# Fills between vector passes, and three groups of gathered lists beside the batches instead of two

## The chip, the core and the metric

The kernel runs on one core of a Trainium2 chip. The metric is the time of one execution on the device in microseconds (us), from the first to the last instruction of the core and what little lies around it. Five engines work side by side, each in the fixed order of its own queue, and wait for one another through semaphores: TensorE (PE, with its weight loads as PEld), VectorE (DVE), ScalarE (ACT), GpSimd (POOL) and SyncE (SP). SP issues the plain transfers of this kernel, POOL all indirect ones: a gather or scatter whose rows are named by a list of indices.

## What is computed

There are 16 graphs with 1024 nodes and 64 channels. `adj` is a dense weighted adjacency in which about 1 in 256 entries is not zero, far more in the first rows than in the last.

```python
# layer 0
h = relu(layernorm(x))
x = x + (adj / max(rowsum(adj), 1)) @ h
# layer 1
h = relu(layernorm(x))
nb = (adj > 0) without the diagonal;  m = nb.sum(-1)
# a node with more than 10 neighbours drops those whose rank is a multiple of ceil(m/2), in both directions
valid = nodes that are left, the node itself among them
agg[c] = 0.25*quantile(h[valid, c], .25) + 0.5*quantile(.., .5) + 0.25*quantile(.., .75)
out = x + (relu((h + agg) @ W1 + b1) @ W2 + b2) * mask
```

The quantiles need each node's neighbours in sorted order, channel by channel.

## The kernel before

**Layer 0, the batches.** For each graph (`front`, then `back`) SP loads eight blocks of 128 rows of `adj`, DVE turns each block into the numbers of its nonzero columns (`max` over four segments, L336), PE transposes it (L341) and multiplies it with `h` (L358). `back` writes the layer's result to two tables in DRAM (`tab` and `own`), and ranks the nodes of the graph by list length with a one-hot permutation (L438, L444), so that lists of like length lie together. The result of four graphs is one record, `rec_g`.

**Layer 1, the groups.** Four graphs make a group, and there are four groups. A group's 4096 nodes lie in 32 tiles of 128 lists. `group` first prepares: it transposes the records, finds keys and indices of every list, gathers one row of `adj` for tile 0 (`gat_rows`), and writes which neighbours the longest lists drop into the table (`tab`, L757). It then makes one job for each class of list length (`CAPS`): ten jobs of 1 to 6 tiles, with 15, 10, 8, 7, 6, 5, 4, 3, 2 and 1 neighbours. A job goes through four steps. `fetch` gathers its rows on POOL, one indirect transfer for each neighbour of each tile (`places`, L481) and one for the node itself (`S`, L481). `sort` runs on DVE: a sorting network of elementwise minimum and maximum between places (L531), then a product with the quantile weights (L544). `layers` is the small perceptron on PE and ACT, which ends in the tile `y` (L590, two buffers). `add` adds the residual on DVE (L629), and `store` scatters `y` to the output, again on POOL (L595). In `pipeline` step s fetches job s+2 (`AHEAD`), stores job s-2, runs the perceptron of job s-1 and sorts job s. Over its ten jobs a group issues 124 gathers of neighbours, 31 of own rows and 31 stores.

**The longest lists.** The 32 longest lists of every graph (tile 0 of the groups) go separately, in four jobs over all graphs, with eight lists of each graph in a job: `long_lists` finds up to 88, 31, 24 and 20 neighbours from whole rows of `adj` (`lat`), and their rows come into `lplaces`.

**The order of work.** The program is written as generators. Each `yield` names a cost, and `weave` always advances the stream that has used the smaller part of its budget; `WAIT` says that a stream can't go on yet. Before, a first stage weaves the batches (budget 480) with groups 0 and 1 (budget 270), where a job's costs are DVE's time. A second stage weaves the longest lists (440) with groups 2 and 3 (270); all four `long_lists` are prepared before the first of their jobs is fetched. A group may start when the fronts of its graphs are written. What the generators write out is then arranged by a scheduler, which gives each engine its fixed order: an instruction without a dependency can stand far ahead of where it was written.

The lines that matter in the profile are these: L481 all gathers, L595 the stores, L491 the first instruction of a sort (`rem`), L531 the passes of the network, L544 the products, L590 and L629 the end of a job.

Of the kernel before, what the change touches and what calls it, by code (L numbers as in the profile page):

```python
# [10 lines left out]
I32 = mybir.dt.int32  # L11
# [24 lines left out]
LONG = (88, 31, 24, 20)  # L36
LSUB = 8
WAIT = "wait"
AHEAD = 2


# [110 lines left out]
def list_path(ctx, tc, x, adj, nodemask, w1, b1, w2, b2, out, go):  # L152
# [24 lines left out]
    ps_s = ctx.enter_context(tc.tile_pool(name="ps_s", bufs=3, space=bass.MemoryType.PSUM))  # L177


    diff = consts.tile([P, P], I32, name="diff")  # L180
    nc.gpsimd.iota(diff, pattern=[[1, P]], base=0, channel_multiplier=-1)
    ident = consts.tile([P, P], F32, name="ident")
    nc.vector.tensor_scalar(ident, diff, 0.0, None, op0=OP.is_equal)
# [17 lines left out]
    nc.vector.tensor_scalar(rev, col, -1.0, float(N), op0=OP.mult, op1=OP.add)  # L201
    zeros = consts.tile([P, N], BF, name="zeros")
    nc.vector.memset(zeros, 0.0)
    place1 = consts.tile([P, P], F32, name="place1")
    nc.vector.tensor_scalar(place1, col[:, :P], 1.0, None, op0=OP.add)
    cls_i = consts.tile([P, CLS, NT], I32, name="cls_i")
    nc.gpsimd.iota(cls_i, pattern=[[-1, CLS], [0, NT]], base=CLS - 1, channel_multiplier=0)
    cls = consts.tile([P, CLS, NT], F32, name="cls")
    nc.vector.tensor_copy(cls, cls_i)
# [41 lines left out]
    adj_rows = adj.rearrange("b i j -> (b i) j")  # L251
    out_rows = out.rearrange("b n c -> (b n) c")

    first = keep.tile([REC, len(LONG), B, LSUB], HF, name="first")
    scatters = []

# [229 lines left out]
    def aggregate(pool, n, T, A, S, keys, node):  # L486

        rem = pool.tile([P, n - 1, T, 2], F32, name="rem2")  # L490
        nc.vector.tensor_tensor(  # L491
            rem, A[:, 1:, :, C:],
            node.unsqueeze(1).unsqueeze(3).to_broadcast([P, n - 1, T, 2]), OP.is_equal,
        )
        gone = pool.tile([P, n - 1, T], F32, name="gone")
        nc.vector.tensor_tensor(gone, rem[:, :, :, 0], rem[:, :, :, 1], OP.max)
        ok = pool.tile([P, n - 1, T], F32, name="ok")
        nc.vector.scalar_tensor_tensor(
            ok, keys.rearrange("p t k -> p k t"), 0.0, gone, op0=OP.is_gt, op1=OP.subtract
        )  # L500
        valid = pool.tile([P, T], F32, name="valid")
        nc.vector.tensor_reduce(valid, ok.rearrange("p k t -> p t k"), AX.X, OP.add)
        ops, count, at = network(n)
        w = weights(pool, count, T, valid)
        vals = A[:, 1:, :, :].rearrange("p k t w -> p (k t) w")[:, :, :C]
        nc.vector.scalar_tensor_tensor(
            vals, gone.rearrange("p k t -> p (k t)").unsqueeze(2).to_broadcast([P, (n - 1) * T, C]),
            HUGE, vals, op0=OP.mult, op1=OP.add,
        )
        Bt = pool.tile([P, n, T, C], F32, name="other", bufs=1)  # L510

        def places(copy, start, step, number):
            if copy == 2:
                return S[:, :, :C].unsqueeze(1)
            src = A if copy == 0 else Bt
            return src[:, start:start + step * (number - 1) + 1:step, :, :C]

        cost = 2.0 + (n - 1) * T * C * 1.05e-3
        for op, ai, aj, dist, run in ops:
            if cost > 8.0:  # L520
                yield cost
                cost = 0.0
            cost += 0.15 + len(run) * T * C * 1.05e-3
            step = run[1] - run[0] if len(run) > 1 else 1
            a = places(ai, run[0], step, len(run))
            c = places(aj, run[0] + dist, step, len(run))
            if op == OP.min:
                dst = places(0 if ai == 1 else 1, run[0], step, len(run))
            else:
                dst = places(0 if aj == 1 else 1, run[0] + dist, step, len(run))  # L530
            nc.vector.tensor_tensor(dst, a, c, op)  # L531

        short = pool is gat
        total = max(count + 1, 4)
        if short:
            prod = pool.tile([P, T, total, C], F32, name="prod", bufs=2)
            if count + 1 < total:
                nc.vector.memset(prod[:, :, count + 1:, :], 0.0)
        for copy in range(2):
            for run in runs_of([k for k in range(count) if at[k] == copy]):  # L540
                step = run[1] - run[0] if len(run) > 1 else 1
                sl = slice(run[0], run[-1] + 1, step)
                src = places(copy, run[0], step, len(run))
                nc.vector.tensor_tensor(  # L544
                    prod[:, :, sl, :].rearrange("p t k c -> p k t c") if short else src, src,
                    w[:, sl, :].unsqueeze(3).to_broadcast([P, len(run), T, C]), OP.mult,
                )
        yield cost + 0.4 + count * T * C * 1.05e-3
        if not short:
            return [  # L550
                [places(at[k], k, 1, 1)[:, 0, t, :] for k in range(count)] + [S[:, t, :C]]
                for t in range(T)
            ]
        nc.scalar.copy(prod[:, :, count, :], S[:, :, :C])

        return [
            [prod[:, t, k:min(k + 2, total), :].rearrange("p k c -> p (k c)")
             for k in (0, *range(4, total, 2), 2)]
            for t in range(T)
        ]  # L560

    def perceptron(terms, mask, T):

        R = terms[0][0].shape[1]
        y = mlp.tile([P, T, CO], F32, name="y", bufs=2)
        for t0 in range(0, T, 4):
            ts = range(t0, min(t0 + 4, T))
            M = len(ts) * P
# [62 lines left out]
        def store(self):  # L631
            store(self.y, self.T, self.nodes_i)

    def pipeline(jobs, ahead):

        J = len(jobs)
        for j in range(min(ahead, J)):
            jobs[j].fetch()
        for s in range(J + 2):
            if s + ahead < J:  # L640
                jobs[s + ahead].fetch()
            if s >= 2:
                jobs[s - 2].store()
            if 1 <= s <= J:
                jobs[s - 1].layers()
            if s < J:
                yield from jobs[s].sort()
            if 1 <= s <= J:
                jobs[s - 1].add()
            yield 0.2  # L650

    def group(g, rec_g):

# [227 lines left out]
    def groups(records, gs):  # L881
        for g in gs:
            while progress["batches"] < (g + 1) * GB:
                yield WAIT
            yield from group(g, records[g])
            yield from pipeline(todo[g], AHEAD)

    def longs(pool):
        for l in range(len(LONG)):
            yield from long_lists(pool, l)  # L890
        while not progress["dropped"]:
            yield WAIT
        yield from pipeline(todo[NG], 2)

    records = []
    with tc.tile_pool(name="lay0", bufs=2) as pool:
        lay0 = batches(pool, records)
        while progress["batches"] < GB - 1:
            next(lay0)
        weave((lay0, 480.0), (groups(records, (0, 1)), 270.0))  # L900
    with tc.tile_pool(name="long", bufs=1) as pool:
        def rest():
            yield from group(2, records[2])
            yield from group(3, records[3])
            progress["dropped"] = True
            yield from pipeline(todo[2] + todo[3], AHEAD)
        weave((longs(pool), 440.0), (rest(), 270.0))


    bad = tiny.tile([P, 1], F32, name="bad")  # L910
# [288 lines left out]
```

## Time and profile before

| | us |
|---|---|
| median of 3 runs (2073.25 to 2082.36) | 2081.86 |
| the profiled execution's own time | 1907.73 |
| its span | 1905.9 |
| DVE busy / POOL busy | 1277.7 / 1183.2 |
| PE busy / PEld busy / ACT busy | 852.7 / 520.7 / 434.3 |
| indirect transfers on POOL: `places`, `lplaces`, `S` of groups, stores of groups | 496, 163, 124, 124 |
| preparation of groups 0, 1, 2 and 3 begins on DVE | 176, 514, 878, 911 |
| first sort of the 88-neighbour lists begins | 1126 |

A group of the profile lists its busy time, its mean duration in ns, and the idle time of the engine ahead of it with what ended that wait. A row of the stage table shows the busy time of each engine in a stretch of the span, with the number of instructions in brackets. A timeline line has its start, its duration, the engine, the source line and, in square brackets, the idle time before it. The busy time of a POOL transfer is its issue on the engine, not the flight of the data.

### The profile page before, as it was taken

To read this page: it belongs to the slowest core of one execution; us is meant where nothing else is said; L and a number is where in the kernel's file an instruction comes from. 1 tells how busy PE (TensorE), PEld (TensorE's weight loads), DVE (VectorE), ACT (ScalarE), POOL (GpSimd) and SP (SyncE) were. 2 spreads that over 40 slices of the span, in tenths; PEclk is the share of its full clock that TensorE was granted. 3 is DMA by queue.
4 is the path that set the end of the run, shared out by engine and by line. 5 is a ranking of instruction groups with operands and counts; after the bars stand their busy time and mean duration, and the time that the engine had idled before them with its cause. 6 is when DMAs were issued, how large, how long until landed. Compare 5 with 4: busy or idle time off the path is not lost.

```text
span 1905.9 us, 15523 instructions
## 1 busy us (share of the span) xinstructions
PE 852.7 (45%) x3724; PEld 520.7 (27%) x3724; DVE 1277.7 (67%) x4747; ACT 434.3 (23%) x1010; POOL 1183.2 (62%) x940
## 2 busy tenths in 40 slices
PE   6898177578973756794002000011163123311275
PEld 4433043245531433452002000011033123301244
DVE  8989799777878998786975036066564776624362
ACT  6654243344441543332000000000001000000021
POOL 0001665775428277744157787788888888878753
PEclk9989587878886787796555555555555556655556
DMA  5645343354342544311111101111111000010100
GB/s 177 184 133 129 96 117 110 94 140 109 96 124 62 144 124 122 84 41 50 37 28 26 27 21 24 27 23 21 21 25 21 14 13 20 14 28 16 27 24 15
DMA packets 116516, 124.32 MB, mean 65 GB/s; under 512 B 84242, under 2 KB 84370, under 8 KB 116418
## 3 DMA queue, kind: packets, MB, share of 16 engines
q1 hardware_dynamic: 85730, 84.15, 15.7%
q0 software_dynamic: 30688, 39.11, 10.0%
q8 instruction: 31, 0.51, 0.1%
q14 instruction: 67, 0.55, 0.1%
HBM read 106.27 MB, written 16.92 MB: 65 GB/s over the span
## 4 chain that ended last, share of the span: by engine, by line
POOL 37%; PE 19%; issue 17%; DVE 15%; DMA 10%; ACT 3%; POOLq 0%; SPq 0%; DVEq 0%; ACTq 0%
POOL places L481 19%; POOL lplaces L481 9%; PE pm L358 6%; POOL S L481 6%; DMA places<-tab,idx 4%; PE pm L444 3%; PE pt L572 3%; POOL out_dram L595 3%; PE pt L341 3%; DMA at<-in_adj_dram 2%; DVE other L531 2%; DVE rec L336 2%; DVE places L531 2%; DMA S<-own,nodes_i 1%; PE ps_small L588 1%
## 5 line engine op out<-in xcount | busy, mean ns | idle before, releaser
L481 POOL DMA_INDIRECT places<-tab,idx x496 | 664.6, 1340 | 214.2 <-issue 140.8
L572 PE MATMUL pt<-ident,prod 128*128 128x128 f32 (+1 forms) x736 | 159.1, 376 | 652.1 <-DVE prod L544 652.1
L572 PEld LDWEIGHTS pt<-ident,prod 128*128 128x128 f32 (+1 forms) x736 | 128.4, 257 | 687.6 <-DVE prod L544 460.6
L358 PE MATMUL pm<-att,h 128*65 128x512 f32 x512 | 244.8, 624 | 6.4 <-ACT att L342 6.4
L595 POOL DMA_INDIRECT out_dram<-y,nodes_i x124 | 131.2, 1058 | 135.2 <-issue 44.6
L481 POOL DMA_INDIRECT S<-own,nodes_i x124 | 189.1, 1525 | 38.4 <-issue 30.2
L481 POOL DMA_INDIRECT lplaces<-tab,lidx x163 | 171.1, 1050 | 49.7 <-issue 49.1
L336 DVE MAX8 rec<-sg 128x8 f16<-128x256 f16 x512 | 188.5, 412 | 1.8 <-issue 1.8
L341 PE MATMUL pt<-ident,at 128*128 128x128 f32 x1024 | 163.0, 306 | 48.3 <-DMA at<-in_adj_dram 30.2
L331 ACT ACTIVATE sg<-at 128x1024 f16<-128x1024 f32 x128 | 135.9, 1061 | 136.7 <-DVE rec L336 124.2
L341 PEld LDWEIGHTS pt<-ident,at 128*128 128x128 f32 x1024 | 132.6, 158 | 85.0 <-issue 41.6
L590 ACT ACTIVATE y<-ps_small,recs 128x64 f32<-128x64 f32 x124 | 30.8, 315 | 535.7 <-DMA out_dram<-y,nodes_i 496.1
L342 ACT COPY att<-pt 128x512 f32<-128x512 f32 x256 | 140.1, 590 | 26.8 <-PE pt L341 25.3
L629 DVE TENSOR_TENSOR y<-y,S 128x64 f32<-128x64 f32 (+4 forms) x44 | 15.0, 343 | 171.3 <-ACT y L590 171.3
L476 DVE TENSOR_TENSOR w<-wu 128x16 f32<-128x16 f32 (+12 forms) x44 | 7.7, 175 | 173.4 <-ACT wu L473 173.4
L481 POOL DMA_INDIRECT gat_rows<-in_adj_dram,nodes_i x4 | 4.4, 1098 | 181.7 <-DVE over L686 176.7
L444 PE MATMUL pm<-perm,rec 128*34 128x512 f16 x256 | 94.2, 482 | 47.7 <-DVE perm L438 46.7
L579 PE MATMUL pm<-ot,w_sb 128*128 128x128 f32 (+3 forms) x112 | 50.5, 551 | 136.0 <-ACT ot L577 136.0
L358 PEld LDWEIGHTS pm<-att,h 128*65 128x65 f32 x512 | 69.8, 144 | 145.1 <-issue 131.4
L531 DVE TENSOR_TENSOR other<-places 128x128 f32<-128x128 f32 (+6 forms) x276 | 91.9, 348 | 0.0
L531 DVE TENSOR_TENSOR other<-lplaces 128x128 f32<-128x128 f32 (+9 forms) x267 | 88.8, 373 | 0.0
L333 DVE TENSOR_TENSOR sg<-sg,rev 128x1024 f16<-128x1024 f16 x128 | 86.9, 681 | 0.0
(194 smaller groups left out, 1671.3 us busy)
## 6 DMA issues: line engine op xcount, KB each, us to landing
at<-in_adj_dram SPq DMA_DIRECT2D x128, 512.0 KB
places<-tab,idx POOLq DMA_INDIRECT x496, 2.5
tab<-h SPq DMA_DIRECT2D x16, 264.0 KB
xt<-in_x_dram SPq DMA_DIRECT2D x16, 256.0 KB
own<-x SPq DMA_DIRECT2D x16, 256.0 KB
own<-h SPq DMA_DIRECT2D x16, 256.0 KB
lplaces<-tab,lidx POOLq DMA_INDIRECT x163, 2.4
S<-own,nodes_i POOLq DMA_INDIRECT x124, 2.6
```

The source lines that it names most:

```text
L331: nc.scalar.activation(sg, at, AF.Sign, accum_out=total[:, t:t + 1])
L333: nc.vector.tensor_tensor(sg, sg, rev, OP.mult)
L336: nc.vector.max(out=rec[:, t, 8 * s:8 * s + 8], in_=segs[:, s, :])
L341: nc.tensor.transpose(pt[:, q * P:(q + 1) * P], at[:, c0:c0 + P], ident)
L342: nc.scalar.copy(att[:, h2 * BPH:(h2 + 1) * BPH, k * P:(k + 1) * P], pt.rearrange("p (q i) -> p q i", i=P),)
L358: nc.tensor.matmul(po[:C + 1, :], st["h0"][:, q, :], st["att"][hf][:, q, :], start=(q == 0), stop=(q == NT - 1),)
L444: nc.tensor.matmul(pr[:REC, :], rec[:, t, :], perm[:, t, :], start=(t == 0), stop=(t == NT - 1))
L481: nc.gpsimd.indirect_dma_start(out=dst, out_offset=None, in_=src, in_offset=bass.IndirectOffsetOnAxis(ap=idx, axis=0),)
L531: nc.vector.tensor_tensor(dst, a, c, op)
L572: nc.tensor.matmul(pt[:term.shape[1], i * P:(i + 1) * P], term, ident, start=(k == 0), stop=(k == len(terms[t]) - 1),)
L579: nc.tensor.matmul(ph[:, :M], w1_sb[:R, :], ot[:R, :M], start=True, stop=True)
L595: ins = nc.gpsimd.indirect_dma_start(out=out_rows, out_offset=bass.IndirectOffsetOnAxis(ap=idx[:, t:t + 1], axis=0), in_=y[:, t, :], in_of ...
```

## The change

Four things are changed.

1. `Breath`: after every 0.8 us of two-operand passes in `aggregate` (L531, L544), as estimated from their sizes, a `memset` of one element in each partition of a tile `idle` of its own is written out on DVE.
2. `pipeline` names other costs: for the groups 1.27 for each indirect transfer that a step issues and nothing for the sort. The long lists keep DVE's costs.
3. The first stage weaves the batches (480) with groups 0, 1 and 2 (730). The second stage has group 3 alone (250) beside the longest lists (440). The 88-neighbour job is fetched as soon as its lists are found and all dropped neighbours are written; the other three `long_lists` are prepared after that.
4. Buffers: `y` has three instead of two. The constants `diff` and `cls_i` share the buffers of `keys` and `idx`, and `place1` becomes a view of `col_f`.

```diff
+BREATH = 0.8
...
-    diff = consts.tile([P, P], I32, name="diff")
+    diff = grp.tile([P, P], I32, name="keys")
...
-    place1 = consts.tile([P, P], F32, name="place1")
-    nc.vector.tensor_scalar(place1, col[:, :P], 1.0, None, op0=OP.add)
-    cls_i = consts.tile([P, CLS, NT], I32, name="cls_i")
+    place1 = col_f[:, 1:]
+    cls_i = grp.tile([P, CLS, NT], I32, name="idx")
...
+    idle = consts.tile([P, 1], F32, name="idle")
+    class Breath:
+        def __init__(self):
+            self.since = 0.0
+        def __call__(self, cost):
+            self.since += cost
+            if self.since > BREATH:
+                nc.vector.memset(idle, 0.0)
+                self.since = 0.0
+    breathe = Breath()
...
             nc.vector.tensor_tensor(dst, a, c, op)
+            breathe(0.07 + len(run) * T * C * 1.05e-3)
...
                     w[:, sl, :].unsqueeze(3).to_broadcast([P, len(run), T, C]), OP.mult,
                 )
+                breathe(0.07 + len(run) * T * C * 1.05e-3)
...
-        y = mlp.tile([P, T, CO], F32, name="y", bufs=2)
+        y = mlp.tile([P, T, CO], F32, name="y", bufs=3)
...
-    def pipeline(jobs, ahead):
+    def pipeline(jobs, ahead, fetched=0, by_pool=True):
         J = len(jobs)
-        for j in range(min(ahead, J)):
+        for j in range(fetched, min(ahead, J)):
             jobs[j].fetch()
         for s in range(J + 2):
+            transfers = 0
             if s + ahead < J:
                 jobs[s + ahead].fetch()
+                transfers += jobs[s + ahead].n * jobs[s + ahead].T
             if s >= 2:
                 jobs[s - 2].store()
+                transfers += jobs[s - 2].T
             if 1 <= s <= J:
                 jobs[s - 1].layers()
+            if by_pool:
+                yield 1.27 * transfers
             if s < J:
-                yield from jobs[s].sort()
+                for cost in jobs[s].sort():
+                    yield 0.0 if by_pool else cost
             if 1 <= s <= J:
                 jobs[s - 1].add()
-            yield 0.2
+            yield 0.0 if by_pool else 0.2
...
     def longs(pool):
-        for l in range(len(LONG)):
-            yield from long_lists(pool, l)
+        yield from long_lists(pool, 0)
         while not progress["dropped"]:
             yield WAIT
-        yield from pipeline(todo[NG], 2)
+        todo[NG][0].fetch()
+        yield 0.0
+        for l in range(1, len(LONG)):
+            yield from long_lists(pool, l)
+        yield from pipeline(todo[NG], 2, fetched=1, by_pool=False)
...
-        weave((lay0, 480.0), (groups(records, (0, 1)), 270.0))
+        weave((lay0, 480.0), (groups(records, range(NG - 1)), 730.0))
...
-            yield from group(2, records[2])
-            yield from group(3, records[3])
+            yield from group(NG - 1, records[NG - 1])
             progress["dropped"] = True
-            yield from pipeline(todo[2] + todo[3], AHEAD)
-        weave((longs(pool), 440.0), (rest(), 270.0))
+            yield from pipeline(todo[NG - 1], AHEAD)
+        weave((longs(pool), 440.0), (rest(), 250.0))
```

## The prediction

> **What bounds the kernel now.** I read the page first: engine shares, the chain of waits, the POOL groups.
>
> ```profile
> PE 852.7 (45%) x3724; PEld 520.7 (27%) x3724; DVE 1277.7 (67%) x4747; ACT 434.3 (23%) x1010; POOL 1183.2 (62%) x940
> POOL 37%; PE 19%; issue 17%; DVE 15%; DMA 10%; ACT 3%; POOLq 0%; SPq 0%; DVEq 0%; ACTq 0%
> L481 POOL DMA_INDIRECT places<-tab,idx x496 | 664.6, 1340 | 214.2 <-issue 140.8
> ```
>
> DVE is the busiest, yet POOL carries the chain. A gather takes 1340 ns on average with 140.8/462 = 0.30 us of issue ahead of it. POOL's timeline late in the span tells what is in that mean:
>
> ```profile
> 1445.03 0.97 POOL L481 DMA_INDIRECT places<-tab,idx  x1 [0.31 <-DMA places<-tab,idx]
> 1446.30 8.46 POOL L481 DMA_INDIRECT places<-tab,idx  x1 [0.30 <-issue]
> 1455.06 0.94 POOL L481 DMA_INDIRECT places<-tab,idx  x1 [0.30 <-issue]
> ...
> 1604.61 30.70 POOL L481 DMA_INDIRECT S<-own,nodes_i  x1 [0.30 <-issue]
> ```
>
> An undisturbed transfer is 0.95 + 0.30 = 1.25 us; some are held, up to 30.70 us. DVE's timeline shows when the 8.46 us one was let go:
>
> ```profile
> 1453.37 0.55 DVE L629 TENSOR_TENSOR y<-y,S 128x384 f32<-128x384 f32 x1
> 1453.84 0.17 DVE L491 TENSOR_TENSOR rem<-places,recs 128x10 f32<-128x10 f32 x1
> 1454.02 0.33 DVE L538 MEMSET prod<- 128x320 f32 x1
> ```
>
> It had only two-operand passes beside it, and ended at 1454.76, 0.74 us after the memset began. The stages, cut where a group's preparation or the 88-neighbour sort begins:
>
> ```profile
> 176.00:514.00 338.00, 227.27 (x1014) 129.74 (x1013) 276.18 (x1009) 130.28 (x296) 207.48 (x186) 0.79 0.41 106
> 514.00:878.00 364.00, 258.38 (x1101) 143.00 (x1100) 293.70 (x1096) 139.18 (x311) 211.28 (x189) 0.80 0.39 99
> 878.00:1126.00 248.00, 15.54 (x80) 12.49 (x76) 131.79 (x477) 6.59 (x26) 145.43 (x146) 0.50 0.14 32
> 1126.00:1906.00 780.00, 206.86 (x906) 163.20 (x906) 417.88 (x1593) 54.81 (x176) 617.11 (x412) 0.55 0.10 21
> ```
>
> The third and the last pair ahead of the clock are DVE and POOL. From POOL's pair follows its account: transfers at 1.25, held time (busy less 0.95 each), and the rest:
>
> | stage | n x 1.25 | held | rest |
> |---|---|---|---|
> | 176-514 | 186: 232 | 31 | 75 |
> | 514-878 | 189: 236 | 32 | 96 |
> | 878-1126 | 146: 182 | 7 | 59 |
> | 1126-1906 | 412: 515 | 226 | 39 |
>
> With the 176 us before, this adds up to 1906. In the last stage POOL is never idle for long and is held for 29% of it. In the first two it has room (rest 171), and DVE is 81% busy.
>
> **What the Trainium skill says.** "SBUF — State Buffer", section "Who interferes with whom": a DVE instruction with two SBUF inputs contends with a GpSimd instruction that reads SBUF, one with at most one input outside the 2-port modes does not, and the lock is exclusive. The holds agree (30.70 us); a memset as a release agrees with the 8.46 us case. The same passage infers that such passes spare descriptor generation; here indirect transfers are held, and the measurement decides. No page says where a scheduler puts an independent instruction.
>
> **The change part by part.**
>
> *Fills.* The program has 572 of them. A one-element memset takes 59 ns (the 32 of `caps`), so 34 us if all were on the path. But a fill depends on nothing except the fill before it, and in the instruction order compiled for DVE the scheduler has put them, it seems, where it expected DVE to be idle: rows of 24, 47 and 49 just ahead of the first sort of groups 0, 1 and 2, 56 ahead of the 88-neighbour sort, 44 near the end. From that sort to the last but one, where the long stretches are, only ten stand. By the durations of the rows (0.07 us + 1.04 ns an element from start to start) the longest stretches of two-operand passes there are 48, 44, 40, 38 and 37 us; before they are 41, 38, 36, 33 and 29. So the fills open nothing; bounds are +34 us, and a gain of all 226 held if they did their work. I take +5, for those in stretches where DVE is late.
>
> *Three groups in the first stage.* A cycle from one preparation to the next has: 189 transfers, 236 us. Held: 25, somewhat under 31 and 32, as DVE now waits for rows at times and leaves the lock. The rest: about 12 from preparation to the first row, as before group 0 (22 us with eight transfers in it); 10 for short waits; and an end in which POOL has only 21 stores (26 us), because in the compiled order the next preparation comes after more layer-0 work: by row durations 65, 80 and 77 us stand between the start of the last job and that preparation, with 10% of idle time (the first 176 us have 18) 70, 87 and 84. That leaves 44, 61 and 58. Cycles: 236 + 25 + 66, 83 and 80 = 327, 344, 341. Stage one ends at 176 + 1012 + 5 = 1193, 315 later than before. Check from DVE, its instructions summed over source lines: 514 us of layer 0 and constants and 3 x (14 of preparation + 90 of sorting) are 826 us of work in 1193, so the order is the bound, not DVE's work.
>
> *Preparation and the 88 gathers.* One group instead of two: about 36 us to the first row (DVE work between by the order, plus the write of `tab`), then 33 + 88 + 2 = 123 transfers, 154, and 2.5 for the landing: 192 instead of 248. The 88 gathers stand behind the same 33 as before, so fetching them first moves nothing; what was behind them, 55 gathers of shorter long lists, is now dealt among group 3's, and costs the same 1.25 each. The sort begins at 1385.
>
> *The last stage.* 931 transfers in all, less 3 x 189 and 131: 233, so 291 us. Held: two-operand passes shrink from 412 to 338 us by the order, so 226 x 338/412 = 185. Rest 39 as before, which is its end. Sum 515: the span ends at 1900.
>
> *Buffers of y.*
>
> ```profile
> ACT y L590 <- DMA out_dram<-y,nodes_i: 496.1, 22, 100.9
> DVE y L629 <- ACT y L590: 171.3, 11, 51.3
> ```
>
> With two buffers ACT waits for stores that stand in POOL's queue behind gathers, and DVE behind ACT. POOL works on meanwhile, free of the lock, so a third buffer gains only where POOL later runs dry: between 0 and 39; I take 12. Shared constants and the missing `place1` pass (under 0.3 us) are at the start beside the first loads: nothing; `diff` is long read when group 0's keys need its buffer.
>
> **Sum.** 1900 - 12 = 1888, with 1.8 around it 1890, against 1907.73: -0.9%. The timed median is 174 us above the profiled execution. If that is in proportion, 2081.86 x 0.991 = 2063; if it is held time (which no run shows), it shrinks with the passes: 1890 + 174 x 0.82 = 2033. I say **2050**. A difference of about 0.5% is what a measurement of this kernel can tell from none.
>
> **The rivals.**
> 1. *Slower: DVE, PE and ACT drag layer 0 behind each group.* Their orders are fixed too, and perceptrons stand among layer-0 work, so when DVE waits for rows, PE and ACT stop as well. For: in 176-878 a batch took 702/12 = 58 us against 176/4 = 44 at the start. If the ends of the three cycles run at 58/44 of the above, 241 becomes 318: +77, 1967, or 2147 on the median's scale. It decides from 18 us in all, 6 a cycle. Against: PE and ACT have idle time here.
> 2. *A better overlap.* With y free DVE sorts earlier, the max8 rows of the later long lists break the 88-neighbour network, and the holds drop to 0.4 of the passes: 135 instead of 185, and 10 less in each cycle: 1810, about 1975.
> 3. *The fills do open the lock*: then the 260 held go to about 60: 1690, about 1845. The compiled order speaks against it.
> 4. *Nothing to see*: the held and idle time only change places, within 0.5% of 2082.
>
> **How the numbers follow.** Rival 1 in some degree has 0.39; rival 4 0.14; faster 0.47, made of the forecast (0.27), rival 2 (0.18) and rival 3 (0.02). The forecast is the likeliest single case; its own range is 2015 to 2071. The whole range has to take in both signs: 1955 to 2165, which leaves out rival 3 and the far ends.
>
> **What would show it.** Right: preparations at about 176, 503, 847 and 1193, the 88-neighbour sort near 1385, POOL transfers over 10 us still in the last stage, fills bunched ahead of first sorts, ACT's wait for stores well under 496. Wrong: preparation of group 3 after 1240 (rival 1), a last stage under 450 us (rival 2), no transfer over 2 us (rival 3).

## The result, and the profile after

The changed kernel is slower: 2173.6 us (median of 4 runs, 2163.12 to 2191.84) against 2077.56 us for the kernel before beside it. The ratio is 1.048, 95% interval 1.039 to 1.056. The forecast was 2050, with a range up to 2165.

One thing has to be known to read any number below: the runs fell on several chips of two kinds. On one kind the kernel before takes 2052 to 2092 us, and wake-ups come late in every trace (shown in experiments 5 and 14); on the other it takes 1892 to 1920, and none does. I call them *late chips* and *prompt chips*. ACT's 256 copies `att`, which wait for transposes of PE, show the difference in every trace: in the eleven prompt ones none begins more than 0.1 us after PE and ACT have finished what came before it; in each of the nine late ones 6 to 13 copies begin over 2 us after, the latest of them 6.6 to 19.2 us. Whether the kind belongs to the chip or to its state at the time is open, since no chip was seen in both. The page of before comes from a prompt chip, the timed runs of the prediction and of the result from late ones. Ratios are always against the kernel before on the same chip, and profiled spans are only compared within a kind.

Page of the change, on a late chip: engines, chain of waits, and the group of the gathers.

```profile
PE 870.2 (40%) x3724; PEld 530.1 (25%) x3724; DVE 1325.7 (61%) x5318; ACT 438.0 (20%) x1010; POOL 1116.6 (52%) x940
...
DVE 23%; POOL 19%; PE 19%; issue 17%; another core or an unknown queue 15%; DMA 4%; ACT 3%; DVEq 0%; SPq 0%; POOLq 0%; ACTq 0%
...
L497 POOL DMA_INDIRECT places<-tab,idx x496 | 574.8, 1159 | 220.7 <-issue 142.3
```

The new entry is "another core or an unknown queue", 15% of the chain; there is no other core. (The late traces hold only half as many semaphore records as the prompt ones, 11,390 against 23,047 for the kernel before, so part of this entry can be a releaser that was not recorded. The late copies above are read from start and end times alone.) POOL is busy for 1116.6 us instead of the 1183.2 on the page of before, and yet the kernel is slower. The stages, cut as in the prediction (length first, then busy time of PE, PEld, DVE, ACT and POOL, with counts):

```profile
173.00:562.00 389.00, 195.29 (x858) 116.69 (x858) 242.45 (x1002) 107.57 (x247) 202.24 (x189) 0.71 0.28 75
562.00:960.00 398.00, 207.17 (x858) 122.69 (x858) 239.41 (x968) 106.71 (x245) 196.52 (x189) 0.68 0.28 73
960.00:1358.00 398.00, 199.07 (x773) 116.90 (x774) 224.12 (x1005) 87.40 (x208) 194.54 (x189) 0.65 0.22 56
1358.00:1621.00 263.00, 15.70 (x53) 11.90 (x52) 103.18 (x434) 5.90 (x25) 153.85 (x160) 0.50 0.12 29
1621.00:2161.00 540.00, 115.37 (x572) 93.22 (x572) 359.92 (x1343) 28.75 (x88) 367.52 (x204) 0.56 0.07 16
```

A cycle takes 389 to 398 us instead of the forecast 327 to 344, although POOL is busy in it for only 195 to 202 us and DVE for 224 to 242. The buffer part did what was forecast: ACT's wait for stores is nearly gone (35.3 us here and 58.3 in run 13 on a prompt chip, against 496.1 on the page of before, which is prompt too). New is that POOL waits for the keys of the second and third preparation. From the list of waits (us in total, times, longest):

```profile
POOL gat_rows L497 <- DVE keys L735: 109.3, 2, 62.2
...
ACT y L608 <- DMA out_dram<-y,nodes_i: 35.3, 1, 35.3
```

The same kernel on a prompt chip (experiment 13) takes 1944.25 us, ratio 1.020 (1.016 to 1.023). Its chain of waits and its stages:

```profile
POOL 42%; DVE 16%; PE 16%; issue 16%; DMA 8%; ACT 2%; SPq 0%; POOLq 0%; DVEq 0%; ACTq 0%
```

```profile
171.00:501.00 330.00, 196.25 (x858) 119.47 (x858) 241.22 (x1002) 106.86 (x247) 213.10 (x189) 0.74 0.33 88
501.00:846.00 345.00, 196.18 (x858) 118.95 (x858) 238.47 (x968) 106.63 (x245) 208.89 (x189) 0.73 0.32 84
846.00:1181.00 335.00, 194.44 (x774) 115.69 (x774) 222.60 (x1006) 86.70 (x210) 202.53 (x189) 0.67 0.27 67
1181.00:1391.00 210.00, 14.39 (x52) 11.67 (x52) 98.10 (x431) 5.25 (x21) 139.63 (x134) 0.50 0.14 29
1391.00:1952.00 561.00, 118.33 (x572) 96.16 (x572) 355.31 (x1343) 28.86 (x88) 437.72 (x230) 0.55 0.08 18
```

Here the landmarks of the forecast are met within 12 us: preparations at 171, 501, 846 and 1181 (forecast 176, 503, 847, 1193), the 88-neighbour sort at 1391 (1385). That the last of these is so close is in part luck: the stage before it began 12 us early and took 18 us more than forecast. The last stage is clearly longer, 561 instead of 515, or 503 with the 12 us of the y buffer taken off.

POOL's account by stage, worked out as in the prediction (transfers at 1.25 us; held, busy less 0.95 each; rest). The cycles column gives the lengths with the rest in brackets:

| kernel, chip | cycles (rest) | preparation to 88-sort | last stage: transfers, held, rest |
|---|---|---|---|
| before, prompt | 338, 364 (75, 96) | 248 | 780: 515, 226, 39 |
| before, late (exp. 1) | 412, 436 (160, 173) | 337 | 724: 420, 199, 105 |
| forecast of the change | 327, 344, 341 (66, 83, 80) | 192 | 515: 291, 185, 39 |
| change, prompt (13) | 330, 345, 335 (60, 79, 76) | 210 | 561: 288, 219, 54 |
| change, late | 389, 398, 398 (130, 145, 147) | 263 | 540: 255, 174, 111 |
| change, DVE's costs, prompt (9) | 309, 290, 283 (47, 27, 30) | 231 | 470: 284, 157, 29 |
| the same, dependent fills, prompt (11) | 309, 302, 276 (46, 40, 23) | 226 | 415: 284, 83, 48 |

### The profile page after: what moved, and what is told of

It is laid out like the page before. It is cut to its first block, busy times and chain, and to the rows that moved or that the text cites. A ratio compares the mean times of both kernels' runs of the same rounds, so it can differ in the third digit from the quotient of the medians.

```text
span 2161.0 us, 16094 instructions
## 1 busy us (share of the span) xinstructions
PE 870.2 (40%) x3724; PEld 530.1 (25%) x3724; DVE 1325.7 (61%) x5318; ACT 438.0 (20%) x1010; POOL 1116.6 (52%) x940
## 4 chain that ended last, share of the span: by engine, by line
DVE 23%; POOL 19%; PE 19%; issue 17%; another core or an unknown queue 15%; DMA 4%; ACT 3%; DVEq 0%; SPq 0%; POOLq 0%; ACTq 0%
POOL places L497 11%; DVE other L547 6%; POOL lplaces L497 6%; PE pm L374 5%; PE pt L590 5%; DVE places L547 3%; PE pt L357 2%; PE pm L460 2%; DVE lplaces L547 2%; DMA at<-in_adj_dram 2%; POOL S L497 2%; DVE rec L352 2%; PE ps_small L606 1%; PE ps_small L603 1%
## 5 line engine op out<-in xcount | busy, mean ns | idle before, releaser
L497 POOL DMA_INDIRECT places<-tab,idx x496 | 574.8, 1159 | 220.7 <-issue 142.3
L590 PE MATMUL pt<-ident,prod 128*128 128x128 f32 (+1 forms) x736 | 167.2, 392 | 795.7 <-DVE prod L561 537.9
L374 PE MATMUL pm<-att,h 128*65 128x512 f32 x512 | 254.2, 647 | 6.0 <-ACT att L358 6.0
L613 POOL DMA_INDIRECT out_dram<-y,nodes_i x124 | 145.2, 1171 | 189.9 <-DVE y L647 55.0
L497 POOL DMA_INDIRECT lplaces<-tab,lidx x163 | 214.5, 1316 | 49.7 <-issue 48.8
L497 POOL DMA_INDIRECT S<-own,nodes_i x124 | 156.4, 1261 | 125.2 <-issue 54.0
L488 ACT ACTIVATE wu<-wu 128x48 f32<-128x48 f32 (+12 forms) x44 | 10.6, 242 | 691.1 <-DVE wu L484 500.4
L547 DVE TENSOR_TENSOR places<-other 128x128 f32<-128x128 f32 (+6 forms) x264 | 86.1, 349 | 59.7 <-remote 52.3
L547 DVE TENSOR_TENSOR other<-places 128x128 f32<-128x128 f32 (+6 forms) x276 | 92.6, 350 | 46.3 <-remote 29.6
L547 DVE TENSOR_TENSOR other<-lplaces 128x128 f32<-128x128 f32 (+9 forms) x267 | 88.6, 370 | 14.7 <-issue 12.9
L454 DVE TENSOR_SCALAR perm<-col_h,pos 128x512 f16<-128x512 f16 x256 | 74.4, 350 | 33.5 <-remote 21.9
L547 DVE TENSOR_TENSOR lplaces<-other 128x128 f32<-128x128 f32 (+8 forms) x272 | 81.9, 346 | 11.3 <-issue 11.3
```

The costliest lines, as they stand in the source:

```text
L374: nc.tensor.matmul(po[:C + 1, :], st["h0"][:, q, :], st["att"][hf][:, q, :], start=(q == 0), stop=(q == NT - 1),)
L454: nc.vector.tensor_scalar(perm[:, t, :], col_h[:, hf * HALF:(hf + 1) * HALF], pos[:, t:t + 1], None, op0=OP.is_equal,)
L497: nc.gpsimd.indirect_dma_start(out=dst, out_offset=None, in_=src, in_offset=bass.IndirectOffsetOnAxis(ap=idx, axis=0),)
L590: nc.tensor.matmul(pt[:term.shape[1], i * P:(i + 1) * P], term, ident, start=(k == 0), stop=(k == len(terms[t]) - 1),)
L613: ins = nc.gpsimd.indirect_dma_start(out=out_rows, out_offset=bass.IndirectOffsetOnAxis(ap=idx[:, t:t + 1], axis=0), in_=y[:, t, :], in_of ...
```

## The experiments

At first the third group's cycle was the suspect, with fills, late wake-ups and held time as rivals; the naming of costs was a rival from run 4 on. Runs 1 to 4 fell on one late chip.

**1. The kernel before, unchanged**, with a profile.

> The kernel before, unchanged, for a second trace. Its profiled execution took 1908 us, its timed ones 2068 to 2082. If late wake-ups (waits put down to another core or an unknown queue, 15% of the chain of the changed kernel and none before) belong to the machine and not to the change, this execution is near 2075 us and has them too, some 150 us in all. If they come from the change, they are absent and the profile is again near 1908 us.

2073.8 us, ratio 1.003 (1.000 to 1.007). Its trace shows "another core or an unknown queue 15%" too, and cycles of 412 and 436 us where the page of before has 338 and 364. So what was new in the page of the change is not due to the change, and the page that the forecast was built on lacked something that the timed runs had.

**2. The change without fills**

```diff
-BREATH = 0.8
+BREATH = 1.0e9
```

> The changed kernel with the fills' threshold at 1e9, so that none is written out. If the order of the work (three groups beside the batches) makes it slower, it stays at 1.04 to 1.05 of before. If the fills do (572 more instructions on DVE, each with a semaphore), it falls to 1.00 to 1.01.

Ratio 1.043 (1.035 to 1.051), not separable from the change. The longest transfer is 41.4 us without fills and 40.2 with them: in this order the fills open nothing of the long stretches.

**3. The fills alone**, on the kernel before.

```diff
             nc.vector.tensor_tensor(dst, a, c, op)
+            breathe(0.07 + len(run) * T * C * 1.05e-3)
```

> The kernel before with the fills alone. By the forecast they open nothing and cost 5 to 34 us: 1.00 to 1.015 of before. If they cost the whole difference: 1.045. If they do let POOL through after all: below 0.95, with no POOL transfer over 3 us late in the span.

Ratio 1.019 (1.011 to 1.028), somewhat over what was expected. That is some 40 us (23 to 57), where all 572 memsets together take 34; in the change itself run 2 finds no such cost. The trace shows a different order, in which held time has become waiting. In the last stage 63 us are held instead of the 199 of run 1, and the longest transfer is 15.8 us instead of 30.7; but from the preparation of group 2 to the end POOL's rest grows from 167 to 300 us. Some of these waits are put down to a fill:

```profile
POOL places L498 <- DVE idle L267: 59.0, 6, 28.7
...
POOL S L498 <- DVE idle L267: 35.1, 5, 27.7
```

261 of the fills stand in this last stage, but none of its 29 transfers over 1.25 us ends where a fill would have let it go (0.86 to 0.95 us after the fill begins, see below on run 11). So they open next to nothing here either. What in the new order costs the 40 us is not settled.

**4. The change with two groups in each stage**

```diff
-        weave((lay0, 480.0), (groups(records, range(NG - 1)), 730.0))
+        weave((lay0, 480.0), (groups(records, range(2)), 487.0))
...
-            yield from group(NG - 1, records[NG - 1])
+            yield from group(2, records[2])
+            yield from group(3, records[3])
...
-        weave((longs(pool), 440.0), (rest(), 250.0))
+        weave((longs(pool), 440.0), (rest(), 500.0))
```

> The changed kernel with two groups beside the batches (budget 487) and two beside the longest lists (500), all else as changed. If the third group in the first stage is what costs, this is 1.00 of before or a little less; if naming GpSimd's time as the cost, which changes the order in every stage, is what costs, it stays at 1.03 to 1.05.

Ratio 1.029 (1.018 to 1.041): most of the loss is there without the third group.

**5. A dense row of gathers beside layer 0 alone.** 120 gathers that nobody reads are added to the kernel before; POOL issues them in the first 160 us, where it had almost nothing to do.

```diff
         while progress["batches"] < GB - 1:
             next(lay0)
+            steps += 1
+            if steps % 4 == 0 and steps <= 32:
+                extra = gat.tile([P, 16, 1, W], F32, name="places", bufs=3)
+                for k in range(15):
+                    gather(extra[:, k, 0, :C], x_rows, row_i[:, k % NT:k % NT + 1])
```

> The kernel before with 120 gathers added that nobody reads (rows of the input into the places buffers), issued by POOL from the start, so that some 150 us of them lie beside the first four batches of layer 0, where POOL had nothing to do. Nothing else is changed. Theory A (a dense row of indirect transfers by itself delays the wake-ups of the other engines, so layer 0 beside a group is slow whatever the order): the preparation of group 0, at 173 to 176 us in every execution so far, comes at 200 to 225, DVE's late waits on its own semaphore in the first 170 us become 20 to 60 us in all, and the time rises by about as much, 25 to 50 us. Theory B (layer 0 is slow beside a group because DVE's and PE's orders mix it with sorts and perceptrons): the preparation stays at 173 to 180, the time within 10 us of before.

Late chip: 2195.99 us, ratio 1.055 (1.048 to 1.062). The preparation of group 0 comes at 308 us instead of 175: during the row layer 0 all but stands still. ACT's copies, and between them PE's transposes (start, duration, idle time before):

```profile
47.03 0.58 ACT L342 COPY att<-pt 128x512 f32<-128x512 f32 x1 [12.43 <-remote]
...
47.67 1.11 PE L341 MATMUL pt<-ident,at 128*128 128x128 f32 x4 [12.74 <-issue]
...
58.22 0.58 ACT L342 COPY att<-pt 128x512 f32<-128x512 f32 x1 [10.61 <-remote]
...
68.72 0.59 ACT L342 COPY att<-pt 128x512 f32<-128x512 f32 x1 [9.91 <-remote]
```

PE goes on as soon as the copy at 47.03 has ended, and its four transposes are done at 48.78; ACT, idle all the while, begins the next copy at 58.22, 9.4 us later. One copy comes every 11 us: a wake-up for eight or nine transfers at 1.25 us. Theory A holds, far beyond the size it gave.

**6. The third group alone**, with DVE's costs as before.

```diff
-        weave((lay0, 480.0), (groups(records, (0, 1)), 270.0))
+        weave((lay0, 480.0), (groups(records, (0, 1, 2)), 405.0))
...
-        weave((longs(pool), 440.0), (rest(), 270.0))
+        weave((longs(pool), 440.0), (rest(), 135.0))
```

> The kernel before with the third group in the first stage (budget 405, group 3 alone in the second with 135) and nothing else of the change: DVE's costs, two y buffers, no fills, all long lists prepared first. Theory A (each group beside batches costs a cycle with some 140 us in which POOL neither transfers nor is held, and the last stage gives back less than a third cycle costs): preparations at about 175, 585, 1000 and 1400, end 2110 to 2160, ratio 1.02 to 1.04. Theory B (the loss comes from naming POOL's time as cost): cycles under 380, ratio 0.98 to 1.01.

Late chip: 2037.54 us, ratio 0.980 (0.975 to 0.985). Theory A, mine until then, falls: the third group is a gain.

**7. POOL's time as cost, alone**: `pipeline` as changed, on the kernel before.

```diff
-        weave((lay0, 480.0), (groups(records, (0, 1)), 270.0))
+        weave((lay0, 480.0), (groups(records, (0, 1)), 487.0))
...
-        weave((longs(pool), 440.0), (rest(), 270.0))
+        weave((longs(pool), 440.0), (rest(), 500.0))
```

> The kernel before with only the costs changed: 1.27 for each indirect transfer and nothing for the sort in the groups, two groups in each stage, budgets 487 and 500 in place of 270. Theory A (the third group is what costs): ratio 0.99 to 1.015, preparations near 175, 590, 1050. Theory B (POOL's time as cost puts more layer-0 work behind each group and costs by itself): ratio 1.02 to 1.03, that of the change with two groups, with second cycle 470 to 490.

Late chip: ratio 1.021 (1.015 to 1.026), second cycle 479 us. Theory B holds.

**8. Fills that can't be moved.** They read the result of the pass before them.

```diff
-                nc.vector.memset(idle, 0.0)
+                nc.vector.tensor_reduce(idle, last, AX.X, OP.max)
...
-            breathe(0.07 + len(run) * T * C * 1.05e-3)
+            breathe(0.07 + len(run) * T * C * 1.05e-3, dst[:, 0, 0:1, :2])
```

> The kernel before with fills that cannot be moved away: after every 0.8 us of two-operand passes a tensor_reduce of two elements of the pass's own result into the tile idle, so that it depends on that pass; in the compiled order some 440 of the 572 stand singly among the passes. Theory A (an opening of one short instruction is enough for a held transfer): no transfer over 5 us, held time in the last stage 40 to 80 instead of 199, cost of the fills there 300 x 0.1 = 30, end 1950 to 2020, ratio 0.94 to 0.98. Theory B (so short an instruction is over before the transfer gets in): held time 150 to 220 as now, and the fills cost, ratio 1.01 to 1.03. Theory C (the holds go, but DVE is late next): held time under 80 and rest in the last stage up by as much, ratio 0.99 to 1.01.

Late chip: 2016.32 us, ratio 0.972 (0.967 to 0.978). Held time in the last stage falls from 199 to 91 us, the longest transfer from 30.7 to 6.6. Theory A holds in kind; 6.6 and 91 are over its bounds of 5 and 80. Unlike in run 3, the held time has not become waiting: from the preparation of group 2 to the end POOL's rest is 176 us, against 167 in run 1 and 300 in run 3.

**9. The change with DVE's costs in the groups**, all else kept.

```diff
-    def pipeline(jobs, ahead, fetched=0, by_pool=True):
+    def pipeline(jobs, ahead, fetched=0, by_pool=False):
...
-        weave((lay0, 480.0), (groups(records, range(NG - 1)), 730.0))
+        weave((lay0, 480.0), (groups(records, range(NG - 1)), 405.0))
...
-        weave((longs(pool), 440.0), (rest(), 250.0))
+        weave((longs(pool), 440.0), (rest(), 135.0))
```

> The changed kernel with one part taken back: a step of a group costs DVE's time again, as before, instead of 1.27 for each transfer, with budgets 405 and 135 for the groups. Three groups, fills as written, three y buffers and the longest lists first stay. Theory A (POOL's time as cost is what turned the third group's gain into a loss, because it pushes layer 0 to the end of each cycle and lets the gathers run in dense rows): cycles of 350 to 375 instead of 389 to 398, layer 0's rows spread over the quarters of a cycle, end 2010 to 2070, ratio to before 0.97 to 1.00. Theory B (the third y buffer, the order of the longest lists, or the fills cause it): ratio 1.02 to 1.05, as the change.

This run fell on a prompt chip: 1753.8 us against 1909.97, ratio 0.919 (0.915 to 0.923), far under what either theory said. With run 13 beside it (ratio 1.020 on the same kind of chip) it isolates the costs and the budgets that go with them: they make the change 1944 instead of 1754.

**10. Third group and dependent fills together**: the edits of 6 and 8 on the kernel before.

> The two parts that won alone, put together: the kernel before with three groups in the first stage (DVE's costs, ratio alone 0.980) and fills that depend on the pass before them (alone 0.972). Theory A (they act in different stages, so they add): ratio 0.945 to 0.957. Theory B (both take from the same held time of the last stage, of which the third group alone left 84 of 199): ratio 0.962 to 0.977.

Prompt chip: ratio 0.923 (0.921 to 0.925). The sum expected was made from late chips and can't be judged by it.

**11 and 16. The change with both parts mended**: DVE's costs as in 9, fills as in 8.

> The changed kernel with two parts mended: DVE's costs in the groups, and fills that depend on the pass before them. It differs from the run with three groups and true fills by the third y buffer and by fetching the longest lists first. Theory A (those two are worth nothing, since POOL's queue is full beside them): within 1% of that run. Theory B (the third buffer frees DVE and the perceptrons): 1 to 2% under it. Theory C (the longest first shuts the other long lists out until late): 1 to 3% over it.

> The change with DVE's costs and fills that depend on the pass before them. On a chip where the kernel before takes about 1910: 1710 as before, ratio 0.90. On a chip where it takes about 2075: theory A (the gains of third group and true fills add there too) ratio 0.94 to 0.96; theory B (third buffer and longest lists first help there as they did where wake-ups are prompt) 0.89 to 0.93; theory C (they turn against it when wake-ups are late) 0.97 to 1.03.

Prompt chips both times: 1709.98 and 1712.11 us, ratios 0.898 (0.894 to 0.903) and 0.899 (0.896 to 0.901). Against run 10 on the same chip this is 1709.98/1762.25 = 0.970, so third buffer and longest lists first are worth 3%: theory B of run 11, somewhat more than it said. How it does on a late chip was not seen.

**13. The change itself on a prompt chip**, with no edit.

> The changed kernel as it is. On a chip where the kernel before takes about 1910 us and its trace has no late wake-ups: theory A (late wake-ups beside dense gathers made the change slower, and the prediction's account holds without them) 1780 to 1890, ratio 0.93 to 0.99, cycles of 320 to 350; theory B (the order by POOL's time is bad in itself) ratio 1.01 to 1.05, cycles of 370 to 400. On a chip where the kernel before takes about 2075: ratio 1.04 to 1.055, as before.

Ratio 1.020 (1.016 to 1.023), with cycles of 330, 345 and 335 us. Each theory is half right: the account of the cycles holds, and the kernel is slower all the same.

**5 again, and paced (12, 14, 15, 18).** Run 14 is run 5 on a prompt chip. The other three put a pause between 72 such gathers:

```diff
+                    rest_i = grp.tile([P, P], I32, name="keys")
+                    for q in range(4):
+                        nc.gpsimd.iota(rest_i, pattern=[[1, P]], base=0, channel_multiplier=-1)
```

> The 120 extra gathers in dense rows beside the first four batches, as before. On a chip where the kernel before takes about 1910: theory A (the hold-up of wake-ups is a property of the chip's state, not of gathers as such) preparation of group 0 at 175 to 185, ratio 0.995 to 1.01; theory B (dense gathers always stop layer 0) preparation near 311, ratio 1.05 to 1.07. On a chip where it takes about 2075: preparation near 311, ratio 1.05 to 1.06.

> The extra gathers beside the first four batches once more, but 72 of them, with four small iota instructions on POOL (0.2 us each) ahead of every one, so that one comes every 2.1 us instead of every 1.25 us and they last some 155 us. The 120 unpaced ones moved the preparation of group 0 from 175 to 311 us, 1.1 us for each gather. Theory A (the wake-ups are held up while POOL issues transfers back to back, and a pause lets them through): preparation at 175 to 195. Theory B (every transfer costs the other engines its time, paced or not): preparation at 245 to 260. Theory C (any busy POOL holds them up): preparation near 310.

> The 72 extra gathers with a pause of four small iotas ahead of each. On a chip where the kernel before takes about 1910: as before, preparation at 175, ratio 1.00. On a chip where it takes about 2075: theory A (a pause between transfers lets the wake-ups through) preparation at 175 to 195, ratio 1.00 to 1.01; theory B (each transfer costs the others its time) 245 to 260, ratio 1.03 to 1.04; theory C (a busy POOL holds them up whatever it does) near 310, ratio 1.05 to 1.07.

> The 72 extra gathers with a pause of four small iotas ahead of each. On a chip where the kernel before takes about 2075: theory A (a pause between transfers lets the wake-ups through) preparation of group 0 at 175 to 195, ratio 1.00 to 1.01; theory B (each transfer costs the others its time) 245 to 260, ratio 1.03 to 1.04; theory C (a busy POOL holds them up whatever it does) near 310, ratio 1.05 to 1.07. On a chip where it takes about 1910: 175 and 1.00 as before.

Run 14: ratio 1.000 (0.998 to 1.002), the preparation at 177. The same program that stops layer 0 on a late chip costs nothing on a prompt one. ACT's timeline of run 14 at the same place:

```profile
39.24 2.58 ACT L342 COPY att<-pt 128x512 f32<-128x512 f32 x5
...
44.12 1.05 ACT L342 COPY att<-pt 128x512 f32<-128x512 f32 x2
...
47.02 0.59 ACT L342 COPY att<-pt 128x512 f32<-128x512 f32 x1
47.81 0.59 ACT L342 COPY att<-pt 128x512 f32<-128x512 f32 x1 [0.21 <-PE pt L341]
```

Nine copies stand between 39 and 48 us here, where run 5 has one at 47.03; the waits are 0.2 us. All three paced runs fell on prompt chips (ratios 1.000, 1.000, 1.001), so they say nothing on whether a pause would help on a late one. That stays open.

**17. Run 11 with the long lists prepared as before**, all four ahead of the first fetch.

```diff
-        yield from long_lists(pool, 0)
+        for l in range(len(LONG)):
+            yield from long_lists(pool, l)
...
-        todo[NG][0].fetch()
-        yield 0.0
-        for l in range(1, len(LONG)):
-            yield from long_lists(pool, l)
-        yield from pipeline(todo[NG], 2, fetched=1, by_pool=False)
+        yield from pipeline(todo[NG], 2)
```

> The mended change (DVE's costs, dependent fills, three groups, three y buffers) with the four long lists all prepared before the first is fetched, as before. It stands between the mended change (ratio 0.898 on a chip where the kernel before takes about 1910) and the kernel with three groups and dependent fills alone (0.923). Theory A (the 3% between them are the third y buffer's): ratio 0.895 to 0.905. Theory B (they are the longest lists' order): 0.918 to 0.928. On a chip where the kernel before takes about 2075 it says nothing on this split; ratio 0.93 to 0.97.

Prompt chip: ratio 0.905 (0.899 to 0.910). Against 0.923 with two buffers of `y` and 0.898 with the longest first: some 1.9 of the 2.5 points between them are the third buffer's (the shared constants with it), and the 0.6 of the order is no more than the intervals allow.

## Why the prediction was wrong

It forecast 1890 us on the scale of the page and 2050 as the median, and the measured values are 1954 (run 13's profiled execution) and 2174. Two steps failed, and about equally: the sum on the page's scale is 64 us short, above all in the last stage's held time and rest, and the step from there to the median, put at 160 us (2050 less 1890), was 220. The first alone turns the small gain into a loss: run 13 is slower where the second plays no part.

**The cycles: right, where wake-ups are prompt.** Three cycles were put at 1012 us and took 1010. The order's end, in which POOL has little to do, was put at 70, 87 and 84 us and took 76, 97 and 91. The mechanism is the one named: POOL waits for the keys of the next preparation, which stands behind layer-0 work. Waits of run 13, then of run 9 with DVE's costs:

```profile
POOL gat_rows L497 <- DVE keys L735: 109.8, 2, 64.1
```

```profile
POOL gat_rows L497 <- DVE keys L735: 21.3, 1, 21.3
```

The prediction took this end for the price of a third group. It is the price of the costs, with the budgets that go with them. A step of a group now pays for its fetches, which lie early in a cycle, and its sorts pay nothing; so `weave` writes layer 0 out late. DVE's `sg` and `rec` instructions of layer 0 (casts left out), counted by quarters of each cycle, are 18, 48, 54, 72 and 18, 50, 32, 94 in the first two cycles of run 13, but 30, 54, 54, 54 and 38, 58, 44, 53 in run 9; the ends shrink to 52, 42 and 42. The cycles are 128 us shorter together (1010 against 882), and 111 of these are rest. The last stage is 91 us shorter too, 62 of them held time. I had both orders' parts in hand but never worked out the third group with the old costs.

**Preparation and the 88 gathers: 210 instead of 192.** 134 transfers stand there instead of 123 (+14), they are held for 12 us for which there was no term, and the rest is 30 instead of 38.

**The last stage: the held term failed.** Transfers were put at 291 (288), held time at 185 (219), the rest at 39 less the 12 of the y buffer (54). Held time was taken in proportion to the two-operand passes. The longest holds go with the longest unbroken stretches instead, and the prediction had the longer ones written down (48, 44 and 40 us against 41, 38 and 36) without using them. POOL's timeline of run 13:

```profile
1560.60 1.04 POOL L497 DMA_INDIRECT places<-tab,idx  x1 [0.30 <-issue]
1561.94 40.21 POOL L497 DMA_INDIRECT places<-tab,idx  x1 [0.30 <-issue]
1602.45 0.95 POOL L497 DMA_INDIRECT places<-tab,idx  x1 [0.30 <-issue]
```

In these 40 us DVE's timeline has passes of L547 and L561 and nothing else. With DVE's costs the same stage has 157 us of held time, still with transfers like these (run 9):

```profile
1321.79 44.01 POOL L497 DMA_INDIRECT lplaces<-tab,lidx  x1 [0.30 <-issue]
1366.10 39.60 POOL L497 DMA_INDIRECT lplaces<-tab,lidx  x1 [0.30 <-issue]
```

**The fills: their place was right, and what they could have done is shown.** Of 572, 63 run in the last stage of run 13, and they open no long stretch. The third rival, that fills open the lock, was true of fills that stay: in run 11 some 343 run in the last stage, and held time is 83. POOL's and then DVE's timeline of run 11:

```profile
1345.20 0.96 POOL L497 DMA_INDIRECT lplaces<-tab,lidx  x1 [0.30 <-issue]
1346.47 1.43 POOL L497 DMA_INDIRECT lplaces<-tab,lidx  x1 [0.30 <-issue]
1348.20 1.16 POOL L497 DMA_INDIRECT lplaces<-tab,lidx  x1 [0.30 <-issue]
```

```profile
1346.59 0.48 DVE L547 TENSOR_TENSOR other<-lplaces 128x320 f32<-128x320 f32 x1
1347.00 0.14 DVE L266 TENSOR_REDUCE idle<-lplaces 128x1 f32<-128x2 f32 x1
1347.06 0.48 DVE L547 TENSOR_TENSOR other<-lplaces 128x320 f32<-128x320 f32 x1
1347.46 0.21 DVE L547 TENSOR_TENSOR other<-other,lplaces 128x64 f32<-128x64 f32 x1
1347.60 0.14 DVE L266 TENSOR_REDUCE idle<-other 128x1 f32<-128x2 f32 x1
1347.66 0.88 DVE L547 TENSOR_TENSOR other<-lplaces 128x320 f32<-128x320 f32 x2
```

The transfer begun at 1346.47 is through at 1347.90, 0.90 us after the fill at 1347.00 began, and none of the neighbours is held for more than half a microsecond. Of the 111 transfers over 1.25 us in this stage, 90 end so, 0.86 to 0.95 us after a fill begins. The Trainium skill, "SBUF — State Buffer", section "Who interferes with whom", says that a DVE instruction with at most one SBUF input does not contend with GpSimd outside the 2-port modes; one `tensor_reduce` of 0.14 us per 0.8 us of passes being enough agrees with that (longest transfer 6.6 us instead of 44.0).

A rival to the single input is left. The prediction read the 8.46 us transfer as let go by a memset. But an undisturbed transfer takes 0.94 us or more, and this one ended only 0.74 us after the memset began; it ended 0.92 us after `rem` (L491) began, a two-operand pass that waits for a semaphore. In the last stage of before, 32 of the 64 transfers over 1.25 us, with 177 of the 226 us held, end 0.86 to 0.95 us after such a waiting two-operand pass begins. Nearly all fills of run 11 (554 of 573) wait as well. So a wait on DVE may be what opens the lock, and no run separates the two.

**The y buffer: a gain as forecast, where it could be told apart.** I took 12 us. On its own in the change it wasn't measured; where POOL's queue is better fed it is worth about 2% (run 17 against run 10, on two chips).

**From the page to the median: the other half.** The 174 us between the page and the timed runs were put down to proportion or held time. They are the difference between the two kinds of chip: on prompt ones the kernel before has a median of 1908.66 us, no more than the 1907.73 of the page. Late wake-ups are the one cause of it that the traces show; what they cost in sum was not added up. From prompt to late, profiled, the change's cycles grow by 59, 53 and 63 us, its preparation by 53, and the last stage shrinks by 21: +209 over the whole span, with 2 us at the start. The kernel before grows by 74 and 72 in its cycles and 89 in the preparation, and its last stage shrinks by 56: +178, with 1 us less at the start. Preparation and last stage belong together here, since on late chips some transfers move from the one to the other: together they grow by 32 us in the change and by 33 before, although less is held in the last stage (174 instead of 219, and 199 instead of 226). So the difference lies in the cycles, where gathers run beside layer 0: three of them cost 175 us more, two of them 146. Of the 77 us between the two profiled spans on late chips (2161 and 2084), 46 exist on prompt chips too, and 31 come with the kind of chip; by the medians it is 96, 36 and 60.

**The first rival** had the sign and nearly the number (2147), and its mark was met: the last preparation came after 1240, at 1358. Its mechanism is the smaller part of what happened. It let the ends of the cycles grow from 241 to 318 us; on late chips they took 73, 102 and 102, which is 277. The part before them, in which gathers run in dense rows and for which it had no term, went from a forecast 771 to 908. That its number came so near is luck.

**Which part did it.** On a prompt chip the change without its costs is 0.919 of the kernel before, with them 1.020. On a late chip the third group alone gives 0.980 and the costs alone 1.021. So three groups pay, and POOL's time as cost takes the whole gain and some more. Mended (run 11), the change beats both kernels, with a ratio of 0.90 on prompt chips.

## What to carry to other kernels

A cost in a hand-written order must say what the order is to spread: here the batches compete with the sorts for DVE, so DVE's time spreads them, and POOL's time sends them behind the gathers. A filler instruction must depend on what it is to stand behind, or a scheduler will move it to where it does nothing; on the kernel before, the free fills even came with an order that cost 40 us. And if the profiled execution differs from the timed median by 9%, no step may be sized on the profile until a second execution shows where the 9% lies.

## What the runs showed of the hardware that was not expected

On a late chip, 120 gathers at 1.25 us each held layer 0 up by 133 us (run 5), with one wake-up of ACT in 11 us; on a prompt chip the same gathers cost nothing (run 14, ratio 1.000). Why chips differ in this is not known. Without gathers the two agree: in the first 170 us of the kernel before, where POOL issues next to nothing, the profiled executions on a late and a prompt chip are within 1 us of each other (preparation at 175 and 176).

One unbroken stretch of two-operand passes held a single indirect transfer for 44.0 us (run 9). The stretch went on: it was some 83 us long and held the next transfer for 39.6, so one transfer got through with no other kind of instruction to let it go; it ended 0.89 us after a pass began that waits for a semaphore. A `tensor_reduce` of two elements, 143 ns on average, is enough of an opening (run 11), though it costs more than twice a one-element `memset` of 59 ns.
